# A sparse graph convolution: lists cut to groups of 32 rows, four tiles side by side, two or three tiles kept on chip

## The chip, the cores and the metric

The kernel runs on one core of a Trainium2 chip. A core has TensorE (PE in the profile, its weight loads apart as PEld), VectorE (DVE), ScalarE (ACT), GpSimd (POOL) and SyncE (SP), and 16 DMA engines that all queues share. What counts is the device time of one execution in microseconds, lower being better. Three timed runs of the kernel before gave 1521.48, 1523.54 and 1525.01; the median is 1523.54.

## The reference

One layer of a graph convolution on a dense-stored, mostly empty adjacency, with residual and layer norm; B = 8, N = 4096 nodes, F = 256 features, all fp32:

```python
HW = einsum('bnf,fo->bno', x, W)
A_norm = relu((A + A.T) * 0.5)
D = sum(A_norm, axis=1)
d = where(D > 0, D ** -0.5, 0)
L = eye(N) - d[:, None] * A_norm * d[None, :]
out = relu(einsum('nm,bmo->bno', L, HW))
return layernorm(x + out)      # mean and variance over F, eps 1e-5
```

Node n is linked to node m with a chance that falls as the root of both numbers, so the first blocks of rows are nearly dense and the last ones nearly empty; `adj` has about 70,000 entries that are not zero.

## The kernel before, in words

**Stage 1.** The adjacency is read in pairs of 512x512 blocks. PE transposes (L423), DVE adds block and transpose (L427, `sym`), ACT takes relu (L431), and DVE's reduce at L432 sums groups of 64 columns into `part`, which gives the degrees and also says which 64-row groups of the result a source row touches. The symmetric block is written to `a_dram`. Beside that, PE forms g = r (x W) for 128 rows at a time (transposes L521, products L532), ACT evicts it, and it goes to `g_dram`: one row of g holds all eight batches, 2048 numbers, 8 KB. The first 128 output rows (`lead`) are multiplied in this stage (L490).

**Lists.** The remaining 31 blocks of 128 output rows are made in 16 units of two blocks each (the last has one), in the order `SEQ` = 1 to 7, 0, 8 to 15. Unit u has the blocks 2u+1 and 2u+2. For each unit the kernel works out on the chip which source rows touch it. `patterns` (L192) gives each source row a code of four bits, one for each 64-row quarter of the unit. `KINDS` names the ten codes for which a unit has tiles of its own (one quarter alone, one block, two quarters), and kind 0 takes what is left over. `CAPS` says how many tiles of 128 source rows each kind has in each unit. `count` (L224) counts by matmuls with a triangle of ones, `place` (L234) turns the counts into positions on DVE and offers rows that do not fit their own kind to wider kinds (`OFFERS`), and `place_rest`, `spread`, `collect` and `index` make the final row numbers. `limit`, `base` and `kinds` are constants, filled by one POOL memset for each kind and unit (L163 to L166). The lists of the first units are made in stage 1, where `due` says after how many pairs of blocks each part is issued; the others are made in stage 2, some units ahead.

**Stage 2.** For each tile POOL issues two indirect DMAs: 128 pieces of adjacency rows (`ga`, L814) and 128 rows of g (L827) into the next of the 12 buffers of the ring (`RING`). One matmul step (L1032) multiplies the tile into its target rows, in four chunks of 512 columns. Tiles that touch only a 64-row half are 64 columns wide as weights, and two of them with different halves are put side by side in one step. In the units named in `HUB` the first 128 rows of g are not listed: that tile stays on chip (`g_hub`), and only its adjacency columns are loaded (L809). A block's result takes four PSUM banks, of the tag `b0` for a unit's first block and `b1` for its second[...]. `steps_of` (L750) orders the steps of a unit.

When the last step of a block is issued, `finish` (L907) issues ACT's eviction (L683); DVE's add to the residual (L693), statistics (L702) and inverse root (L715 to L721) come one half-width of matmul work later and its normalisation (L726) three. After a unit's first block is finished, `lists` (L952) takes two `b0` banks for the matmuls of later units' lists (L226, L227, L302, L303, L356), and DVE reads them (L184, L188, L189 and others). These two banks are the third and fourth chunk of the next unit's first block. `after(n, ...)` says how much matmul work must be issued before a piece is: n counts half-widths of 64 columns, and `run_later` (L843) counts them down. The order on each engine is the order of issue that this gives.

Of the kernel before, what the change touches and what calls it, by code (L numbers as in the profile page):

```python
# [15 lines left out]
U32 = mybir.dt.uint32  # L16

# [3 lines left out]
KINDS = [3, 1, 2, 4, 8, 12, 5, 10, 9, 6, 0]  # L21

ONE = slice(1, 5)

OFFERS = [
    (0, (1, 4), (3, 12)),
    (0, (2, 8), (3, 12)),
    (1, (1, 2), (5, 10)),
    (1, (4, 8), (5, 10)),
    (2, (1, 2), (9, 6)),  # L30
    (2, (4,), (6,)),
    (2, (8,), (9,)),
]
# [3 lines left out]
HUB = {0, 1, 3, 6, *range(8, 15)}  # L37

CAPS = [
    [2, 3, 3, 3, 2, 1, 2, 1, 2, 1, 6],  # L40
    [1, 3, 3, 3, 2, 1, 1, 1, 2, 1, 4],
    [1, 3, 3, 2, 2, 1, 2, 2, 1, 1, 3],
    [1, 3, 3, 3, 2, 1, 1, 1, 1, 1, 2],
    [1, 3, 3, 2, 2, 2, 1, 1, 1, 1, 2],
    [1, 3, 3, 2, 2, 1, 1, 1, 1, 1, 2],
    [1, 3, 3, 2, 2, 1, 1, 1, 1, 1, 1],
    [1, 3, 3, 2, 2, 1, 1, 1, 1, 0, 2],
    [1, 1, 2, 2, 2, 1, 1, 1, 2, 1, 1],
    [1, 2, 2, 2, 2, 1, 1, 1, 1, 1, 1],
    [1, 2, 2, 2, 2, 1, 1, 1, 1, 1, 1],  # L50
    [1, 2, 2, 2, 2, 0, 1, 1, 1, 1, 1],
    [1, 2, 2, 2, 2, 1, 1, 1, 1, 0, 1],
    [1, 2, 2, 2, 2, 1, 1, 1, 1, 0, 1],
    [1, 1, 2, 2, 2, 1, 1, 1, 1, 0, 1],
    [0, 4, 4, 0, 0, 0, 0, 0, 0, 0, 1],
# [4 lines left out]
def kernel(  # L60
# [37 lines left out]
    QU = 4  # L98
    HOLD = 10
    RING = 12  # L100
# [4 lines left out]
    mid = KINDS.index(4), KINDS.index(5)  # L105
# [9 lines left out]
    part = const.tile([P, NB, N // Q], F32, name="part")  # L115
# [39 lines left out]
    carry = const.tile([P, NK, NB], F32, name="carry")  # L155
# [3 lines left out]
    kinds = const.tile([P, NK], F32, name="kinds")  # L159
    limit = const.tile([P, NU, NK], F32, name="limit")  # L160
    base = const.tile([P, NU, NK], F32, name="base")
    for k in range(NK):
        nc.gpsimd.memset(kinds[:, k : k + 1], float(KINDS[k] or -1))  # L163
        for u in range(NU):
            nc.gpsimd.memset(limit[:, u, k : k + 1], float(CAPS[u][k] * P))
            nc.gpsimd.memset(base[:, u, k : k + 1], float(first[u][k] * P + 1))  # L166

    own = const.tile([P, QU, 2], F32, name="own")
    nc.vector.memset(own, 0.0)
    for s in range(QU):  # L170
        h = slice((s % 2) * Q, (s % 2 + 1) * Q)
        nc.vector.memset(own[h, s, s // 2 : s // 2 + 1], 1.0)
# [19 lines left out]
    def patterns(u):  # L192

        used = ipool.tile([P, QU, NB], F32, tag="used", name=f"used_{u}", bufs=1)
        nb = blocks(u)
        if nb == 1:
            nc.vector.memset(used, 0.0)
        lo = (2 * u + 1) * 2
        nc.vector.tensor_scalar(
            used[:, : 2 * nb],  # L200
            part[:, :, lo : lo + 2 * nb].rearrange("p m s -> p s m"),
            0.0,
            None,
            ALU.is_gt,
        )
        diag = used[:, :, 2 * u + 1 : 2 * u + 1 + nb]
        nc.vector.tensor_tensor(diag, diag, own[:, :, :nb], ALU.max)
        two = ipool.tile([P, 2, NB], F32, tag="two", name=f"two_{u}", bufs=1)
        uv = used.rearrange("p (b h) m -> p b h m", b=2)
        nc.vector.scalar_tensor_tensor(two, uv[:, :, 1], 2.0, uv[:, :, 0], ALU.mult, ALU.add)  # L210
        pat = ipool.tile([P, NB], F32, tag="pat", name=f"pat_{u}")
        nc.vector.scalar_tensor_tensor(pat, two[:, 1], 4.0, two[:, 0], ALU.mult, ALU.add)
        if u in HUB:
            nc.vector.memset(pat[:, :1], 0.0)
        kind = ipool.tile([P, NK, NB], BF16, tag="kind", name=f"kind_{u}")
        nc.vector.tensor_tensor(
            kind,
            pat.unsqueeze(1).to_broadcast([P, NK, NB]),
            kinds.unsqueeze(2).to_broadcast([P, NK, NB]),
            ALU.is_equal,  # L220
        )
        plan[u] = pat, kind
# [6 lines left out]
    def at_once(*kinds):  # L229

        at = [KINDS.index(k) for k in kinds]
        return slice(at[0], at[-1] + 1, at[-1] - at[0] or 1)

    def place(u, tot, low):  # L234

        pat, kind = plan[u]
        pos, incl = scan(tot, low, NK * NB, f"k{u}")  # L240
        yield
        pos = pos.rearrange("p (k m) -> p k m", k=NK)

        n = ONE.stop - ONE.start
        total = ipool.tile([P, NK], F32, tag="total", name=f"total_{u}", bufs=1)
        nc.vector.tensor_copy(total, incl.rearrange("p (k m) -> p k m", k=NK)[:, :, NB - 1])
        free = ipool.tile([P, NK], F32, tag="free", name=f"free_{u}", bufs=1)
        nc.vector.tensor_tensor(free, total, limit[:, u], ALU.min)
        nc.vector.tensor_add(free, free, base[:, u])
        nc.vector.tensor_tensor(total, total, limit[:, u], ALU.max)  # L250
        ends = ipool.tile([P, NK], F32, tag="ends", name=f"ends_{u}", bufs=1)
        nc.vector.tensor_add(ends, base[:, u], limit[:, u])
        upto = ipool.tile([P, 4, n], F32, tag="upto", name=f"upto_{u}", bufs=1)
        nc.vector.tensor_copy(upto[:, 0], limit[:, u, ONE])
# [858 lines left out]
```

## Time and profile before

| what | value |
|---|---|
| timed runs, median of 3 (lowest to highest) | 1523.54 us (1521.48 to 1525.01) |
| profiled execution: span from first to last instruction | 1527.5 us |
| stage 1 / stage 2 within it | 0 to 594.9 / 594.9 to 1514.2 us, then the last block's end |
| PE, PEld busy | 1441.2, 763.6 us |
| DVE busy | 983.6 us |
| ACT, POOL busy | 369.0, 682.0 us |
| DMA | 564.50 MB in 216714 packets, mean 370 GB/s |
| gathers and other POOL DMAs (queue q0) | 304.94 MB, 50.4% of 16 engines' span |
| matmuls of stage 2 (L1032) | 2872 records as g,ga and 176 with the kept tile |
| indirect gathers of g (L827) and of a (L814) | 268 each, 1101 and 1090 ns on POOL |

The profile is of one execution, and its span is 4 us above the median of the timed ones. Busy time of PE is not PE at its peak: matmuls are pipelined, and their ends are modelled, so neighbours overlap in the records.[...]

### The profile page before, as it was taken

To read this page: it belongs to the slowest core of one execution; us is meant where nothing else is said; L and a number is where in the kernel's file an instruction comes from. 1 tells how busy PE (TensorE), PEld (TensorE's weight loads), DVE (VectorE), ACT (ScalarE), POOL (GpSimd) and SP (SyncE) were. 2 spreads that over 40 slices of the span, in tenths; PEclk is the share of its full clock that TensorE was granted. 3 is DMA by queue.
4 is the path that set the end of the run, shared out by engine and by line. 5 is a ranking of instruction groups with operands and counts; after the bars stand their busy time and mean duration, and the time that the engine had idled before them with its cause. 6 is when DMAs were issued, how large, how long until landed. Compare 5 with 4: busy or idle time off the path is not lost.

```text
span 1527.5 us, 19332 instructions
## 1 busy us (share of the span) xinstructions
PE 1441.2 (94%) x6440; PEld 763.6 (50%) x6440; DVE 983.6 (64%) x3015; ACT 369.0 (24%) x462; POOL 682.0 (45%) x1051
## 2 busy tenths in 40 slices
PE   5999999989989989999999999999999999999995
PEld 5778777767767754433343343333433433333331
DVE  4676578888646463055568769569137688898534
ACT  3655554535434450010100100100010010001111
POOL 3002010010303316666667666666556676656653
PEclk9999999989999999999999999999999999999998
DMA  9999999999879898999999999999979999999995
GB/s 340 365 366 401 393 379 365 359 369 354 344 248 367 332 390 354 401 395 418 361 393 372 402 409 365 393 403 389 384 278 406 346 394 403 405 393 366 379 405 195
DMA packets 216714, 564.50 MB, mean 370 GB/s; under 512 B 16550, under 2 KB 104918, under 8 KB 180134
## 3 DMA queue, kind: packets, MB, share of 16 engines
q0 software_dynamic: 54224, 304.94, 50.4%
q1 hardware_dynamic: 93472, 126.89, 23.8%
q10 hardware_dynamic: 68912, 131.37, 22.7%
q8 instruction: 54, 0.88, 0.2%
q14 instruction: 52, 0.43, 0.1%
HBM read 443.61 MB, written 136.34 MB: 380 GB/s over the span
## 4 chain that ended last, share of the span: by engine, by line
PE 68%; DMA 14%; DVE 9%; issue 5%; POOL 2%; ACT 2%; ACTq 0%; DVEq 0%; POOLq 0%
PE py L1032 49%; PE pg L532 8%; DMA g<-g_dram,gi 6%; PE lead L490 5%; DMA a_dram<-sym 5%; DVE sym L427 3%; PE xtr L521 2%; PE tr L423 2%; DVE part L432 2%; DMA xin<-in_x_dram 2%; DMA ga<-a_dram,ai 1%; ACT sym L431 1%; PE lists L356 1%; ACT xt L522 1%; POOL g L827 0%
## 5 line engine op out<-in xcount | busy, mean ns | idle before, releaser
L1032 PE MATMUL py<-g,ga 128*64 128x512 f32 (+1 forms) x2872 | 813.0, 600 | 18.4 <-DMA g<-g_dram,gi 8.0
L1032 PEld LDWEIGHTS py<-g,ga 128*64 128x64 f32 (+1 forms) x2872 | 293.1, 151 | 525.1 <-issue 493.1
L827 POOL DMA_INDIRECT g<-g_dram,gi x268 | 294.9, 1101 | 219.1 <-PE py L1032 79.1
L814 POOL DMA_INDIRECT ga<-a_dram,ai x268 | 292.0, 1090 | 109.5 <-issue 76.8
L683 ACT ACTIVATE y<-py,minus_r 128x512 f32<-128x512 f32 x120 | 79.9, 687 | 812.3 <-PE py L1032 659.8
L693 DVE TENSOR_TENSOR xr<-xr,y 128x2048 f32<-128x2048 f32 x31 | 71.1, 2294 | 269.1 <-ACT y L683 267.2
L532 PE MATMUL pg<-w_sb,xt 128*128 128x256 f32 x1024 | 232.0, 385 | 5.2 <-ACT xt L522 5.2
L427 DVE TENSOR_TENSOR sym<-tr,adj 128x512 f32<-128x512 f32 x256 | 162.7, 683 | 96.9 <-PE tr L423 80.2
L532 PEld LDWEIGHTS pg<-w_sb,xt 128*128 128x128 f32 x1024 | 195.6, 194 | 33.4 <-ACT xt L522 5.6
L432 DVE TENSOR_REDUCE part<-sym 128x32 f32<-128x2048 f32 x64 | 145.5, 2279 | 62.0 <-ACT sym L431 62.0
L423 PE MATMUL tr<-ident,adj 128*128 128x128 f32 x1024 | 138.4, 285 | 30.6 <-DVE sym L427 19.2
L431 ACT ACTIVATE sym<-sym 128x2048 f32<-128x2048 f32 x64 | 122.6, 1916 | 129.9 <-DVE sym L427 117.5
L452 POOL TENSOR_TENSOR r<-e,neg_half 128x4 f32<-128x4 f32 x8 | 8.3, 1039 | 317.9 <-DVE e L451 236.5
L423 PEld LDWEIGHTS tr<-ident,adj 128*128 128x128 f32 x1024 | 118.6, 146 | 60.4 <-DVE sym L427 32.1
L521 PE MATMUL xtr<-ident,xin 128*128 128x128 f32 x512 | 72.4, 288 | 18.0 <-DVE sym L427 16.5
L702 DVE BATCH_NORM_STATS2 stats<-xr 128x6 f32<-128x256 f32 x256 | 87.0, 413 | 1.1
L726 DVE TENSOR_SCALAR xr<-xr,mv,root 128x256 f32<-128x256 f32 x248 | 83.6, 409 | 0.1
L490 PE MATMUL lead<-gt,strip 128*128 128x512 f32 x176 | 83.0, 598 | 0.0
L522 ACT COPY xt<-xtr 128x512 f32<-128x512 f32 x128 | 68.1, 591 | 46.7 <-PE xtr L521 46.0
L542 ACT ACTIVATE gt<-pg,r 128x512 f32<-128x512 f32 x88 | 60.6, 688 | 74.8 <-PE pg L532 72.3
L1032 PE MATMUL py<-g_hub,ga 128*128 128x512 f32 x176 | 77.3, 592 | 0.0
L521 PEld LDWEIGHTS xtr<-ident,xin 128*128 128x128 f32 x512 | 59.0, 146 | 34.9 <-DVE sym L427 26.4
(142 smaller groups left out, 825.8 us busy)
## 6 DMA issues: line engine op xcount, KB each, us to landing
adj<-in_adj_dram SPq DMA_DIRECT2D x64, 1024.0 KB
a_dram<-sym ACTq DMA_DIRECT2D x64, 1024.0 KB
out_dram<-xr SPq DMA_DIRECT2D x31, 1024.0 KB
xr<-in_x_dram ACTq DMA_DIRECT2D x29, 1024.0 KB
xin<-in_x_dram SPq DMA_DIRECT2D x44, 512.0 KB
g_dram<-gt ACTq DMA_DIRECT2D x22, 1024.0 KB
xin<-in_x_dram POOLq DMA_DIRECT2D x20, 512.0 KB
g_dram<-held ACTq DMA_DIRECT2D x10, 1024.0 KB
```

The source lines that it names most:

```text
L423: ins = nc.tensor.transpose(pt[:, c * P : (c + 1) * P], tji[:, c, a * P : (a + 1) * P], ident)
L427: nc.vector.tensor_add(sym[:, a, :], pt, tij[:, a, :])
L431: nc.scalar.activation(sym, sym, AF.Relu, scale=0.5)
L432: nc.vector.tensor_reduce(part[:, i * A : (i + 1) * A, j * S // Q : (j + 1) * S // Q], sym.rearrange("p a (c q) -> p a c q", q=Q), AX.X, A ...
L490: nc.tensor.matmul(lead[c], lhsT=strip, rhs=g[:, c * S : (c + 1) * S], start=not done, stop=len(done) == NB - 1, skip_group_check=True,)
L521: nc.tensor.transpose(pt[:, k, c, :], xin[b // H][:, b % H + k, c * P : (c + 1) * P], ident)
L532: ins = nc.tensor.matmul(pg[:, k * FO : (k + 1) * FO], lhsT=xt[:, b + k, c, :], rhs=w_sb[:, c, :], start=(c == 0), stop=(c == FC - 1),)
L702: nc.vector.bn_stats(stats[:, b, :], z[:, b, :])
L726: nc.vector.tensor_scalar(z[:, b, :], z[:, b, :], mv[:, b, 0:1], rstd[:, b : b + 1], ALU.subtract, ALU.mult,)
L814: nc.gpsimd.indirect_dma_start(out=at if both else at[:, :P], out_offset=None, in_=a_pairs if both else a_rows, in_offset=bass.IndirectOff ...
L827: nc.gpsimd.indirect_dma_start(out=gt, out_offset=None, in_=g_dram, in_offset=bass.IndirectOffsetOnAxis(ap=gi[:, t : t + 1], axis=0), boun ...
L1032: nc.tensor.matmul(py[2 * u + 1 + b][c][rows, :], lhsT=at[:, off + rows.start : off + rows.stop], rhs=gt[:, c * S : (c + 1) * S], start=ne ...
```

## The change

A unit's lists now go down to groups of 32 rows. There are eight groups in a unit, a source row's code has eight bits, and there are 15 kinds: one group alone (eight of them, 1 to 128), a block (15, 240), two 64-row halves (51, 204, 60, 195) and 0 for the rest. A tile of a single group has 32 columns as weights, and four of them, one for each group of a block, make one step. `CAPS` is new for every unit. `HUBS` says for each unit how many of the first tiles of g (128 rows each) stay on chip: three, two, or none in the last unit. The ring has 11 buffers instead of 12, the pool of adjacency rows 14 as before (`RING` + 3), and kept tiles take no buffer of the ring: `gather_ahead` issues gathers until the ring is full. In stage 1 `keep` sums groups of 32 columns (`sums`), marks which are not zero (`uses`, one byte each) and sums again to `part`, one number for each row and 512 columns. `patterns` works out the code of eight bits, the code of four halves and the code of two blocks. `place` offers rows in two rounds of operations on all eight single kinds. `steps_of` begins a unit with four-wide steps and tiles of its first block, then mixes kept tiles, half pairs and the rest, and ends with the second block's own. `run_later` counts widths down in 64ths as before, a 32-column matmul as half.

```diff
-KINDS = [3, 1, 2, 4, 8, 12, 5, 10, 9, 6, 0]
...
-OFFERS = [
-    (0, (1, 4), (3, 12)),
-    (0, (2, 8), (3, 12)),
-    (1, (1, 2), (5, 10)),
-    (1, (4, 8), (5, 10)),
-    (2, (1, 2), (9, 6)),
-    (2, (4,), (6,)),
-    (2, (8,), (9,)),
-]
+KINDS = [15, 1, 4, 2, 8, 16, 64, 32, 128, 240, 51, 204, 60, 195, 0]
...
-HUB = {0, 1, 3, 6, *range(8, 15)}
+HUBS = [3] * 4 + [2] * 11 + [0]
...
 CAPS = [
-    [2, 3, 3, 3, 2, 1, 2, 1, 2, 1, 6],
...
+    [2, 2, 1, 2, 1, 1, 1, 1, 1, 2, 1, 1, 1, 2, 5],
+    [2, 2, 2, 1, 1, 1, 1, 2, 2, 1, 1, 1, 1, 1, 3],
+    [1, 1, 2, 2, 1, 2, 1, 1, 2, 1, 1, 1, 1, 1, 2],
+    [1, 1, 1, 1, 1, 1, 1, 1, 1, 1, 1, 1, 1, 1, 2],
+    [1, 1, 1, 2, 2, 2, 2, 1, 1, 1, 1, 1, 1, 1, 1],
+    [1, 1, 1, 2, 2, 1, 1, 1, 1, 1, 1, 1, 1, 1, 1],
+    [1, 1, 1, 1, 1, 1, 1, 1, 1, 1, 1, 1, 1, 1, 1],
+    [1, 1, 1, 2, 2, 2, 1, 1, 1, 1, 1, 1, 0, 1, 1],
+    [0, 1, 1, 1, 1, 1, 1, 1, 1, 1, 1, 1, 1, 0, 2],
+    [1, 1, 1, 1, 1, 1, 1, 1, 1, 1, 1, 1, 1, 0, 1],
+    [1, 1, 1, 1, 1, 1, 1, 1, 1, 1, 1, 1, 1, 0, 1],
+    [1, 1, 1, 1, 1, 1, 1, 1, 1, 1, 0, 0, 1, 0, 2],
+    [0, 1, 1, 1, 1, 1, 1, 1, 1, 1, 1, 1, 1, 0, 1],
+    [1, 1, 1, 1, 1, 1, 1, 1, 1, 1, 1, 1, 0, 0, 1],
+    [1, 1, 1, 1, 1, 1, 1, 1, 1, 1, 0, 0, 0, 0, 2],
+    [1, 2, 2, 2, 2, 0, 0, 0, 0, 0, 0, 0, 0, 0, 0],
...
     Q = 64
-    QU = 4
+    E = 32
+    QU = P // E
+    NE = 2 * QU
     HOLD = 10
-    RING = 12
+    RING = 11
     EPS = 1e-5
     NK = len(KINDS)
     tiles = [sum(caps) for caps in CAPS]
     first = [[sum(caps[:k]) for k in range(NK)] for caps in CAPS]
-    mid = KINDS.index(4), KINDS.index(5)
+    mid = KINDS.index(16), KINDS.index(51)
+    NL = NK - 1
     tmax = max(tiles)
 
...
-    part = const.tile([P, NB, N // Q], F32, name="part")
+    uses = const.tile([P, NB, N // E], U8, name="uses")
+    part = const.tile([P, NB, NS], F32, name="part")
...
-    kinds = const.tile([P, NK], F32, name="kinds")
-    limit = const.tile([P, NU, NK], F32, name="limit")
-    base = const.tile([P, NU, NK], F32, name="base")
-    for k in range(NK):
-        nc.gpsimd.memset(kinds[:, k : k + 1], float(KINDS[k] or -1))
+    kinds = const.tile([P, NL], F32, name="kinds")
+    limit = const.tile([P, NU, NL], F32, name="limit")
+    base = const.tile([P, NU, NL], F32, name="base")
+    singles, pairs, whole = slice(1, 1 + NE), slice(10, 14), slice(0, 10, 9)
+    codes = [1, *KINDS[singles], 2, 17, 68, 20, 65]
+    for k in range(NL):
+        nc.gpsimd.memset(kinds[:, k : k + 1], float(codes[k]))
         for u in range(NU):
             nc.gpsimd.memset(limit[:, u, k : k + 1], float(CAPS[u][k] * P))
             nc.gpsimd.memset(base[:, u, k : k + 1], float(first[u][k] * P + 1))
...
     def patterns(u):
 
-        used = ipool.tile([P, QU, NB], F32, tag="used", name=f"used_{u}", bufs=1)
+        def t(shape, name, dtype=F32, **kw):
+            return ipool.tile(shape, dtype, tag=name, name=f"{name}_{u}", **kw)
+
+        def weave(out, pairs_of, by):
+            nc.vector.scalar_tensor_tensor(out, pairs_of[:, :, 1], by, pairs_of[:, :, 0], ALU.mult, ALU.add)
+
+        used = t([P, NE, NB], "used", bufs=1)
         nb = blocks(u)
         if nb == 1:
             nc.vector.memset(used, 0.0)
-        lo = (2 * u + 1) * 2
-        nc.vector.tensor_scalar(
-            used[:, : 2 * nb],
-            part[:, :, lo : lo + 2 * nb].rearrange("p m s -> p s m"),
-            0.0,
-            None,
-            ALU.is_gt,
+        lo = (2 * u + 1) * QU
+        nc.vector.tensor_copy(
+            used[:, : QU * nb], uses[:, :, lo : lo + QU * nb].rearrange("p m s -> p s m")
         )
         diag = used[:, :, 2 * u + 1 : 2 * u + 1 + nb]
         nc.vector.tensor_tensor(diag, diag, own[:, :, :nb], ALU.max)
-        two = ipool.tile([P, 2, NB], F32, tag="two", name=f"two_{u}", bufs=1)
-        uv = used.rearrange("p (b h) m -> p b h m", b=2)
-        nc.vector.scalar_tensor_tensor(two, uv[:, :, 1], 2.0, uv[:, :, 0], ALU.mult, ALU.add)
-        pat = ipool.tile([P, NB], F32, tag="pat", name=f"pat_{u}")
-        nc.vector.scalar_tensor_tensor(pat, two[:, 1], 4.0, two[:, 0], ALU.mult, ALU.add)
-        if u in HUB:
-            nc.vector.memset(pat[:, :1], 0.0)
-        kind = ipool.tile([P, NK, NB], BF16, tag="kind", name=f"kind_{u}")
-        nc.vector.tensor_tensor(
-            kind,
-            pat.unsqueeze(1).to_broadcast([P, NK, NB]),
-            kinds.unsqueeze(2).to_broadcast([P, NK, NB]),
-            ALU.is_equal,
-        )
+        if HUBS[u]:
+            nc.vector.memset(used[:, :, : HUBS[u]], 0.0)
+        several = t([P, NB], "several", bufs=1)
+        nc.vector.tensor_reduce(several, used.rearrange("p s m -> p m s"), AX.X, ALU.add)
+        two = t([P, QU, NB], "two", bufs=1)
+        weave(two, used.rearrange("p (b h) m -> p b h m", h=2), 2.0)
+        four = t([P, 2, NB], "four", bufs=1)
+        weave(four, two.rearrange("p (b h) m -> p b h m", h=2), 4.0)
+        pat = t([P, NB], "pat")
+        nc.vector.scalar_tensor_tensor(pat, four[:, 1], 16.0, four[:, 0], ALU.mult, ALU.add)
+        nc.vector.tensor_scalar(two, two, 1.0, None, ALU.min)
+        ones_q = t([P, 2, NB], "ones_q", bufs=1)
+        weave(ones_q, two.rearrange("p (b h) m -> p b h m", h=2), 4.0)
+        quarter = t([P, NB], "quarter", bufs=1)
+        nc.vector.scalar_tensor_tensor(quarter, ones_q[:, 1], 16.0, ones_q[:, 0], ALU.mult, ALU.add)
+        nc.vector.tensor_scalar(four, four, 1.0, None, ALU.min)
+        block = t([P, NB], "block", bufs=1)
+        nc.vector.scalar_tensor_tensor(block, four[:, 1], 2.0, four[:, 0], ALU.mult, ALU.add)
+        nc.vector.scalar_tensor_tensor(block, several, 1.0, block, ALU.is_gt, ALU.mult)
+        kind = t([P, NL, NB], "kind", BF16)
+        for ks, code in ((singles, pat), (pairs, quarter), (whole, block)):
+            n = kinds[:, ks].shape[1]
+            nc.vector.tensor_tensor(
+                kind[:, ks],
+                code.unsqueeze(1).to_broadcast([P, n, NB]),
+                kinds[:, ks].unsqueeze(2).to_broadcast([P, n, NB]),
+                ALU.is_equal,
+            )
         plan[u] = pat, kind
...
+        upto = ipool.tile([P, 3, NE], F32, tag="upto", name=f"upto_{u}", bufs=1)
+        nc.vector.tensor_copy(upto[:, 0], limit[:, u, singles])
+        off = ipool.tile([P, 3, NE], F32, tag="off", name=f"off_{u}", bufs=1)
+        nc.vector.tensor_copy(off[:, 0], base[:, u, singles])
+
+        def by_place(a):
+            return a.rearrange("p (b r i) -> p r i b", b=2, r=2)
+
+        def offer(s, at, to):
+            has, shift = by_place(upto[:, s]), by_place(off[:, s + 1])
+            then = by_place(upto[:, s + 1])
+            left, end, wants = free[:, to], ends[:, to], by_place(total[:, singles])
+            has, shift, then, wants = (a[at] for a in (has, shift, then, wants))
+            if len(at) == 2:
+                left, end = (a.rearrange("p (b i) -> p i b", b=2) for a in (left, end))
+            nc.vector.tensor_sub(shift, left, has)
+            nc.vector.tensor_sub(then, end, shift)
+            nc.vector.tensor_tensor(then, then, wants, ALU.min)
+            nc.vector.tensor_add(left, then, shift)
+
+        every = slice(None)
+        for h in range(2):
+            offer(0, (every, h), pairs)
+        for h in range(2):
+            for i in range(2):
+                offer(1, (every, h, i), whole)
...
         def keep(i, j, sym, diag):
             nc.scalar.activation(sym, sym, AF.Relu, scale=0.5)
-            nc.vector.tensor_reduce(
-                part[:, i * A : (i + 1) * A, j * S // Q : (j + 1) * S // Q],
-                sym.rearrange("p a (c q) -> p a c q", q=Q),
-                AX.X,
-                ALU.add,
+            rows = slice(i * A, (i + 1) * A)
+            sums = stat1.tile([P, A, S // E], F32, tag="sums", name=f"sums_{i}_{j}")
+            nc.vector.tensor_reduce(sums, sym.rearrange("p a (c q) -> p a c q", q=E), AX.X, ALU.add)
+            nc.vector.tensor_scalar(
+                uses[:, rows, j * S // E : (j + 1) * S // E], sums, 0.0, None, ALU.is_gt
             )
+            nc.vector.tensor_reduce(part[:, rows, j], sums, AX.X, ALU.add)
...
+        def side_by_side(*kinds):
+            n = max(len(of[k]) for k in kinds)
+            return [[(k, of[k][c]) for k in kinds if c < len(of[k])] for c in range(n)]
+
+        pairs = side_by_side(51, 204) + side_by_side(60) + side_by_side(195)
+        rows = side_by_side(0)
+        held = [[(0, -1 - h)] for h in range(HUBS[u])]
+        n = max(len(held), len(pairs), len(rows))
+        mixed = [s for c in range(n) for s in held[c : c + 1] + pairs[c : c + 1] + rows[c : c + 1]]
+        return (
+            side_by_side(1, 2, 4, 8)
+            + side_by_side(15)
+            + mixed
+            + side_by_side(240)
+            + side_by_side(16, 32, 64, 128)
+        )
 
...
-        tc.tile_pool(name="rows", bufs=RING + 2) as apool,
+        tc.tile_pool(name="rows", bufs=RING + 3) as apool,
...
-        for n in range(RING):
-            gather(n)
-        n = RING
+        asked = eaten = done_tiles = 0
+
+        def gather_ahead():
+            nonlocal asked
+            while asked < len(order):
+                fetched = len(ring_tiles)
+                if asked - done_tiles >= RING + 2 or (order[asked][2] >= 0 and fetched - eaten >= RING):
+                    break
+                gather(asked)
+                asked += 1
+
+        gather_ahead()
...
-            for k, t in step:
-                gather(n)
-                n += 1
-            run_later(sum(1 + (rows == slice(0, P)) for _, rows, _, _ in work))
+            done_tiles += len(step)
+            eaten += sum(t >= 0 for _, t in step)
+            gather_ahead()
+            run_later(sum((rows.stop - rows.start) / Q for _, rows, _, _ in work))
```

## The prediction, made before the changed kernel was run

> **What bounds the kernel now.** I read the page's busy shares first, then its costliest groups, then the span cut into stages, then the instructions at single unit changes. From the page (engine rows: busy tenths in 40 slices; groups: busy us, mean ns, idle before and what ended it):
>
> ```profile
> span 1527.5 us, 19332 instructions
> ...
> PE   5999999989989989999999999999999999999995
> DVE  4676578888646463055568769569137688898534
> DMA  9999999999879898999999999999979999999995
> ...
> L1032 PE MATMUL py<-g,ga 128*64 128x512 f32 (+1 forms) x2872 | 813.0, 600 | 18.4 <-DMA g<-g_dram,gi 8.0
> ...
> L432 DVE TENSOR_REDUCE part<-sym 128x32 f32<-128x2048 f32 x64 | 145.5, 2279 | 62.0 <-ACT sym L431 62.0
> ```
>
> TensorE and the DMA engines are both near full. Stage 2 by groups of units (window, its length, busy and count of PE, PEld, DVE, ACT, POOL, then clock, DMA share, GB/s):
>
> ```profile
> 594.90:1040.70 445.80, 435.86 (x1733) 166.14 (x1734) 283.41 (x1074) 36.38 (x56) 299.61 (x277) 0.99 1.01 392
> 1040.70:1145.50 104.80, 104.80 (x360) 40.98 (x358) 44.57 (x173) 5.04 (x8) 61.90 (x60) 1.00 0.92 344
> 1145.50:1345.30 199.80, 199.28 (x851) 76.09 (x850) 163.12 (x634) 21.56 (x33) 134.64 (x119) 1.00 1.00 389
> 1395.60:1514.20 118.60, 112.86 (x418) 41.38 (x414) 62.15 (x217) 13.69 (x21) 61.33 (x58) 0.99 0.94 359
> ```
>
> PE is busy 98% there and the DMA share is 1.0 outside unit 0 (the second line). The first matmul starts of a step are 429 ns apart though each is recorded as 592 ns, so a slot (one tile, or one set of tiles side by side, four chunks of 512 columns in two passes) costs 8 x 0.429 = 3.43 us. Counted from the caps in the code: 250 slots x 3.435 = 859 us; list matmuls 16 x 1.24 = 20; the rest of the 919.3 us of stage 2, about 40, is waiting: some 7 for DVE to read the lists' banks, 33 for tiles.
>
> How a unit change looks when only one step stands between the lists and the next unit, units 11 to 12, on PE and on DVE (start, length, what):
>
> ```profile
> 1340.93 0.95 PE L356 MATMUL lists<-val,hot 128*128 128x28 bf16 x32
> 1341.81 5.37 PE L1032 MATMUL py<-g,ga 128*64 128x512 f32 x24
> 1349.35 1.59 PE L1032 MATMUL py<-g,ga 128*64 128x512 f32 x4 [2.17 <-DVE pos_k L188]
> ```
>
> ```profile
> 1337.96 2.29 DVE L693 TENSOR_TENSOR xr<-xr,y 128x2048 f32<-128x2048 f32 x1 [4.46 <-ACT y L683]
> ...
> 1348.78 0.52 DVE L188 TENSOR_TENSOR pos_k<-incl_k,lists 128x352 f32<-128x352 f32 x1
> 1349.33 0.52 DVE L189 TENSOR_TENSOR pos_k<-pos_k,lists 128x352 f32<-128x352 f32 x1
> ```
>
> The first block's last matmul is at 1336.6; add, statistics, root and list reading end on DVE at 1349.85, 13.2 us later. The two banks of the lists are chunks 2 and 3 of the next unit's first block, so its first step took 6.7 us instead of 3.43: 3.2 lost.
>
> In stage 1 DVE is full in the middle:
>
> ```profile
> 215.00:365.00 150.00, 135.94 (x735) 105.61 (x734) 132.55 (x390) 69.55 (x80) 9.41 (x20) 0.95 0.99 360
> 240.00:280.00 40.00, 38.70 (x207) 28.96 (x206) 39.09 (x134) 18.44 (x23) 0.00 (x0) 1.00 1.00 364
> ```
>
> At the start DVE stands behind POOL's memsets of constants, from the list of waits (total, times, longest):
>
> ```profile
> DVE ends L252 <- POOL base L166: 12.2, 1, 12.2
> ```
>
> **What the Trainium skill says.** "TensorE: Matmul & The Clock Gate", Measured speedup vs the span model: tiles placed side by side start about 4 ns apart and three 32-column tiles gave 2.38 times. The trace of before has pairs only: their matmuls start 7 ns apart and a pair takes one tile's time; four are not shown. "VectorE: DVE Perf Modes", The TRN2 errata: an fp32 tensor_tensor takes (N+151)/0.96 ns; the trace agrees (512 columns: 691 against 0.684 us; 352: 524 against 0.52). "DMA: Bandwidth & Descriptors", Issuing engines are not separate DMA queues: the trace agrees in so far as POOL's gathers and the other queues together fill the same 16 engines to 1.0.
>
> **The change part by part.** *Stage 1, constants.* 14 listed kinds instead of 11, each 1 + 2x16 memsets: 462 instead of 363. They run one every 34 ns, and the `ends` of the first unit waits for number 433 instead of 334: +3.4 us ahead of the first `sym`. DMA drops to 220 GB/s at 15-20 us since no buffer comes free, so I count all 3.4.
> *Stage 1, DVE.* `keep` gains a tensor_scalar and a small reduce (rows of like size 0.17-0.26 with overlap: about 0.4 together) x64 = 26 us, of which 18 lie in 215-365: 7. `patterns` there, four times, is about 16 operations for 7: +1.8 each = 7; `place` has 24 small operations for 28 but 448-wide rows for 352 (+0.1 each) and 256-wide for 128 (+0.13): +0.65 x4 = 2.6. Together 17 into a stretch with 17.5 us idle on DVE, but less than 1 us idle of each 40 in the two full parts, which make up over half of it. I charge 10.5 of 17; ends: 4 and 17. Before 215 DMA and after 365 PE hide the rest; without that cover the other 46 x 0.4 = 18 us would show.
> *Stage 2, slots.* By the new caps: 252 gathered tiles for 268, 34 uses of kept tiles for 11, 241 slots for 250: -9 x 3.43 = -31 us, if four tiles cost what one does.
> *Stage 2, DMA.* Rows gathered plus kept tiles loaded: 29,634+384 for 32,174+128 rows of 8 KB: -18.7 MB, adjacency tiles +0.8 MB: at 387 GB/s -46 us of transfer. It shows only as shorter waits for tiles, since PE is the fuller engine: PE's work is then 828+20, transfers about 862. I take 33 to 25 us, -8. Against it stand a ring of 11 and steps that need four tiles at once: the first step starts two gathers (2.6 us each on POOL) later.
> *Stage 2, list reading.* The lists go out when two half-widths have run after the first block's end. Before, three steps mostly follow that end (one of kind 12, two pairs), so two stand between lists and next unit: the 13.2 us chain is just covered by 3x3.43+1.24+1.7 (two chunks) = 13.3. After, at the ends of units 3, 5, 6 and 8 to 12, kind 240 and one four-wide step follow: one stands between, and the cover is 9.8. The chain grows by 0.4 (448 columns in three operations). Stall 3.2 to 3.8 at each of eight changes, less the one existing: 8x3.5-3.2 = +25. Reads queue behind L693 and root, and the out-normalise behind them; nothing on PE waits for that. Ends: 0 if DVE gets there sooner, 30.
> *Stage 2, DVE.* Busy about 42 of the 46-53 us of a late unit; +2.5 to 4 (patterns, reading) brings it to the 46 of a 13-slot unit: +4, ends 0 and 20.
> Sum: 3.4+10.5-31-8+25+4 = +4 on the profiled 1527.5, 1531. That execution's span is 4 us over the median of the timed runs, 1523.5; so 1528 for the median.
>
> **The rivals.** (a) *Faster: the stalls replace waits for tiles.* Gathers go on while PE stands at a list reading, so 28 us of standing and 46 us less transfer can leave almost no wait for tiles: 33 to 5, -28 instead of -8; with stage 1's operations falling into gaps (4 instead of 10.5) the sum is 3.4+4-31-28+25+4 = -23: 1500. Its place is the ring between POOL's gathers and PE; it decides once waits for tiles fall under 18 us, where the sum reaches -3. For it: transfers of 862 us against 828+20+28 of PE. Against: the ring holds 11 tiles, under three four-wide steps, and DMA was already at a share of 1.0 beside a full PE. (b) *DVE becomes the bound* of stage 1's middle (all 17) and of units 8 to 14 (20): +27, 1549. For: 39.1 of 40 busy. Against: DVE idles in earlier units. (c) *Slower by tiles: four tiles do not run as one.* About 37 steps are four wide; at two at a time they add 37 x 3.43 = 127, part of it in place of tile and list waits: +60 to +100, 1590-1625. It decides from 0.1 of a slot (13 us) on. The skill's 2.38 of 3 would make it 0.26 x 37 x 3.43 = 33, 1560. (d) *Nothing moves*: savings and stalls cancel to within 0.2%, about 3 us, which is what a measurement here can tell.
>
> **Numbers.** My forecast (1515-1541) 0.44, (a) 0.28, (b) 0.18, (c) 0.10. Within 0.2% come 0.13 from the lower part of the forecast's own range and from (d), which lies in it; faster 0.26 of (a) and 0.06 of the forecast = 0.32; slower the rest, 0.55. Range 1500 to 1556: it takes in (a)'s centre and (b).
>
> **What would show it.** Matmul starts of a four-wide step some 7 ns apart in fours, 429 ns to the next four, or else (c). Idle PE before chunks 2 and 3 of units 4, 6, 7 and 9 to 13, ended by `pos_k`; if it is there and gather waits are under 18 us, (a). The first `sym` at 18 instead of 14.6 us; stage 1 ending near 609 instead of 595; stage 2 near 909 us. Waits for tiles above 33 us in stage 2, or DVE at 100% in units 8 to 14, would make the forecast too low.

## The result, and the profile after

The changed kernel takes 1547.37 us (median of four runs, 1545.46 to 1549.99) where before takes 1523.27 (1521.48 to 1525.01): a ratio of 1.0162, 95% interval 1.0141 to 1.0183. It is 24 us slower. The forecast was 1528 in a range of 1500 to 1556; the sign was right, the size (24 us for 4) was not.

The page of the changed kernel, its rows and groups as before:

```profile
span 1543.8 us, 19779 instructions
...
PE   5999998989897989899999999999999999999994
...
DMA  8999999999988899978998999999968999999995
...
L1067 PE MATMUL py<-g,ga 128*32 128x512 f32 (+2 forms) x2600 | 638.5, 613 | 32.2 <-DMA g<-g_dram,gi 19.0
...
L1067 PE MATMUL py<-g_hub,ga 128*128 128x512 f32 x544 | 239.2, 593 | 0.0
```

More of the matmuls use kept tiles (544 records for 176). Idle time ahead of the step's matmuls is longer, 32.2 us for 18.4, and most of it ends with a gather of g. Gathered and kept bytes fell from 304.94 to 287.61 MB on the gathers' queue, and the mean rate from 370 to 354 GB/s with them: fewer bytes, in more time.

Stage 2 by groups of units, columns as in the prediction:

```profile
613.50:1070.10 456.60, 441.56 (x1838) 168.82 (x1838) 302.52 (x1109) 39.17 (x57) 309.63 (x278) 0.99 0.95 360
1070.10:1172.70 102.60, 101.58 (x360) 42.81 (x364) 43.06 (x164) 4.76 (x7) 54.21 (x54) 0.98 0.84 315
1172.70:1373.50 200.80, 194.49 (x846) 75.95 (x841) 175.74 (x656) 21.97 (x33) 131.24 (x118) 0.98 1.00 385
...
1418.50:1530.40 111.90, 103.78 (x412) 39.45 (x404) 65.50 (x236) 13.71 (x21) 62.40 (x57) 0.94 0.96 372
```

Stage 1 ends at 613.5 instead of 594.9: +18.6. Stage 2 takes 916.9 instead of 919.3: -2.4. What lies behind it is 13.4 in both. The nine saved slots (31 us) are gone inside stage 2. Counted from the caps, none of them is in units 1 to 7 (121 slots for 120): unit 0 has two fewer, units 8 to 15 eight. In units 1 to 7 and in unit 0 the DMA share has dropped (0.95 and 0.84; it was 1.01 and 0.92): here bytes were saved while PE was the fuller engine. In units 8 to 11, on the third line, it is 1.00.

The waits that carry this, from the lists of waits of the changed kernel (total, times, longest), and from its timeline the start of stage 2 on PE:

```profile
PE py L1067 <- DMA g<-g_dram,gi: 19.0, 12, 2.6
...
PEld py L1067 <- DVE pos_k L183: 16.4, 7, 3.5
DVE ends L253 <- POOL base L161: 16.0, 1, 16.0
```

```profile
617.26 3.59 PE L1067 MATMUL py<-g,ga 128*32 128x512 f32 x26 [1.68 <-DMA g<-g_dram,gi]
622.93 1.02 PE L1067 MATMUL py<-g,ga 128*32 128x512 f32 x2 [2.07 <-DMA g<-g_dram,gi]
626.39 8.14 PE L1067 MATMUL py<-g,ga 128*32 128x512 f32 x19 [2.45 <-issue]
```

The first two steps of unit 1 take 11.6 us over their two slots; in before they started without a wait.

The two profiled executions are 16.3 us apart, the medians 24. A run of the changed kernel with a span of 1543.8 is listed at 1545.46 us, so the profiled execution of before (span 1527.5) stands for about 1529, 6 above its median, and that of the changed kernel 2 below its own. Three kernels below that have the stage 2 of before, untouched, spent 909.0, 911.2 and 912.7 us in it where the profiled execution of before spent 919.3: units 2, 3 and 7 were longer in it (7 in two of the three comparisons), so its waits for tiles there were probably unlucky ones.

### The profile page after: what moved, and what is told of

The parts are those of the page before. It is cut to its first block, busy times and chain, and to the rows that moved or that the text cites. A ratio compares the mean times of both kernels' runs of the same rounds, so it can differ in the third digit from the quotient of the medians.

```text
span 1543.8 us, 19779 instructions
## 1 busy us (share of the span) xinstructions
PE 1428.1 (93%) x6536; PEld 764.4 (50%) x6536; DVE 1038.3 (67%) x3199; ACT 370.9 (24%) x462; POOL 686.6 (44%) x1143
## 3 DMA queue, kind: packets, MB, share of 16 engines
q0 software_dynamic: 52512, 287.61, 47.7%
## 4 chain that ended last, share of the span: by engine, by line
PE 47%; DMA 24%; issue 14%; DVE 8%; POOL 5%; ACT 2%; ACTq 0%; POOLq 0%; DVEq 0%
PE py L1067 31%; DMA g<-g_dram,gi 14%; PE pg L549 7%; DMA ga<-a_dram,ai 4%; DMA a_dram<-sym 3%; PE tr L439 3%; DVE sym L443 2%; PE lead L507 2%; PE xtr L538 2%; POOL ga L840 2%; POOL g L853 2%; DVE sums L450 2%; ACT sym L447 1%; DMA xin<-in_x_dram 1%; DMA g_dram<-held 1%
## 5 line engine op out<-in xcount | busy, mean ns | idle before, releaser
L1067 PE MATMUL py<-g,ga 128*32 128x512 f32 (+2 forms) x2600 | 638.5, 613 | 32.2 <-DMA g<-g_dram,gi 19.0
L1067 PEld LDWEIGHTS py<-g,ga 128*32 128x32 f32 (+2 forms) x2600 | 224.2, 140 | 432.3 <-issue 386.8
L853 POOL DMA_INDIRECT g<-g_dram,gi x252 | 289.3, 1148 | 204.2 <-PE py L1067 99.8
L840 POOL DMA_INDIRECT ga<-a_dram,ai x252 | 284.9, 1130 | 117.0 <-issue 73.0
L1067 PE MATMUL py<-g_hub,ga 128*128 128x512 f32 x544 | 239.2, 593 | 0.0
L450 DVE TENSOR_REDUCE sums<-sym 128x64 f32<-128x2048 f32 x64 | 145.3, 2277 | 58.8 <-ACT sym L447 58.8
L1067 PEld LDWEIGHTS py<-g_hub,ga 128*128 128x128 f32 x544 | 103.2, 190 | 130.8 <-issue 127.2
L497 POOL DMA_DIRECT2D xin<-in_x_dram x20 | 15.2, 762 | 155.8 <-PE xtr L538 139.7
## 6 DMA issues: line engine op xcount, KB each, us to landing
xin<-in_x_dram SPq DMA_DIRECT2D x44, 512.0 KB, 10.4
g_dram<-held ACTq DMA_DIRECT2D x10, 1024.0 KB, 11.6
```

Of the source, the lines that this page charges most:

```text
L450: nc.vector.tensor_reduce(sums, sym.rearrange("p a (c q) -> p a c q", q=E), AX.X, ALU.add)
L840: nc.gpsimd.indirect_dma_start(out=at if both else at[:, :P], out_offset=None, in_=a_pairs if both else a_rows, in_offset=bass.IndirectOff ...
L853: nc.gpsimd.indirect_dma_start(out=gt, out_offset=None, in_=g_dram, in_offset=bass.IndirectOffsetOnAxis(ap=gi[:, t : t + 1], axis=0), boun ...
L1067: nc.tensor.matmul(py[2 * u + 1 + b][c][rows, :], lhsT=at[:, off + rows.start : off + rows.stop], rhs=gt[:, c * S : (c + 1) * S], start=ne ...
```

## The experiments

Experiments 1, 5, 6 and 8 ran on a chip on which before took 1531.0 us, experiments 2, 3 and 7 beside a before of 1524.4 and the others beside one of 1523.4; so ratios to before are compared, not times. The edits are shown shortened.

**1. The memsets in unit order.**

```diff
-    for k in range(NL):
-        nc.gpsimd.memset(kinds[:, k : k + 1], float(codes[k]))
-        for u in range(NU):
+    for u in SEQ:
+        for k in range(NL):
+            if u == SEQ[0]:
+                nc.gpsimd.memset(kinds[:, k : k + 1], float(codes[k]))
```

> The changed kernel with the same 462 memsets in another order: all constants of the first unit first, then unit by unit. Theory: DVE's first sym waits for the memset of the first unit's last constant, so it starts soon after the first transposes (7.8 us) instead of at 18.8, the gap of the DMA engines at 17 to 22 us closes, and about 9 us are saved: 1538. Rival: the start is bound by DMA or the loss is made up later; then only 0 to 4 us are saved, 1543 to 1547.

Measured: 1548.17 us, ratio 1.0109 (1.0092 to 1.0126), against 1.0162 of the changed kernel: 0.53% of 1531 or 8 us, with intervals that leave some 4 us either way. From the timeline of DVE in this run:

```profile
3.42 0.17 DVE L254 TENSOR_TENSOR ends<-base,limit 128x14 f32<-128x14 f32 x1 [0.89 <-POOL base L162]
...
8.88 0.69 DVE L444 TENSOR_TENSOR sym<-tr,adj 128x512 f32<-128x512 f32 x1 [0.96 <-PE tr L440]
```

The gate is gone: the first `sym` waits for PE at 8.88 us instead of for a memset until 18.8. But the trace keeps less of it than the ratio: against before, the 41st `sym` is 0.7 us late instead of 5.2, the 249th 15.2 instead of 17.6, and stage 2 starts at 610.8 instead of 613.5. The gate is shown; its worth is some 3 us by the trace and 8 by the times, which differ by no more than the intervals allow.

**2. The same edit in before.**

> The kernel before with its 363 memsets in unit order, first unit first. Theory: before has the same gate, at 14.6 us instead of 18.8; its first sym comes at about 8.6 and 5 us are saved. Rival: e1 gained by something else than the gate; then nothing here.

Measured: 1520.36 us, ratio 0.998 (0.9967 to 0.9992), 3 us. The first `sym` comes at 8.7 us, 5.9 earlier; at 17 us the lead is 2.6, from 80 us on 0.8 to 1.9. So of a gate of 6 us a third or less lasts. This is the fastest version seen: its interval ends just below the time of before.

**3. `keep` alone, in before.**

```diff
-            nc.vector.tensor_reduce(part[...], sym by 64, AX.X, ALU.add)
+            nc.vector.tensor_reduce(sums, sym by 32, AX.X, ALU.add)
+            nc.vector.tensor_scalar(uses, sums, 0.0, None, ALU.is_gt)
+            nc.vector.tensor_reduce(part[...], sums by 2, AX.X, ALU.add)
```

> The kernel before with keep's new operations alone: sums of 32 columns, a comparison whose result nothing reads, and the sums of 64 from them; lists and stage 2 as before. Theory: of the +10 us between 220 and 350 us about half is keep's two extra operations, so 4 to 7 us slower than before. Rival: the list operations are all of it and keep's fall into gaps: within 2 us of before.

Measured: 1531.44 us, ratio 1.0048 (1.0032 to 1.0063), 7 us. In its trace `sym` falls back by 1.2 to 1.8 us up to 222 us, by 4.8 at 357, and stage 2 starts at 600.4 instead of 594.9. The rival (within 2 us) is out: two small operations on each of 64 blocks cost some 5 us by the trace and 5 to 10 by the interval of the times. One difference to the changed kernel remains: here the sums are kept in buffers that `patterns` and the list making use too (`used`, `way`), so part of it could be waiting for them; that was not tried apart.

**4. The list operations alone, in before.** `patterns` of the first four units gets ten more operations that work on `used` and whose results nothing reads.

```diff
+            for out in (x[:, 64:320], x[:, 64:320]):
+                nc.vector.scalar_tensor_tensor(out, wide, 2.0, wide, ALU.mult, ALU.add)
+            nc.vector.tensor_reduce(x[:, :32], x[:, 64:320] by 8, AX.X, ALU.add)
+            for n in (128, 64, 32, 32, 32):
+                nc.vector.scalar_tensor_tensor(x[:, :n], row[:, :n], 2.0, row[:, :n], ALU.mult, ALU.add)
+            for n in (128, 64):
+                nc.vector.tensor_scalar(x[:, :n], row[:, :n], 1.0, None, ALU.min)
```

> The kernel before with ten idle DVE operations in patterns of the first four units, 2.8 us a unit, like those that the change adds; their results are not used. Theory: DVE's list operations stand on the path in stage 1, so all of the 11 us show: stage 2 starts 8 to 11 us later and before becomes 8 to 11 us slower. Rival: a gap takes them, under 4 us; then the rest of the 19 us of stage 1 has another cause.

Measured: 1525.6 us, ratio 1.0008 (0.9991 to 1.0025); the trace shows stage 1 3.8 us longer. The theory that list operations show in full fell; the rival, under 4 us, held. What differs in the changed kernel is seen at 230 us of its own PE timeline:

```profile
237.84 3.71 PE L439 MATMUL tr<-ident,adj 128*128 128x128 f32 x16 [6.14 <-DVE sym L443]
```

Here DVE runs some twenty operations, most of them of `patterns` and one a reduce of 2.28 us, between two `sym`; PE waits 6.14 us for the next one. The longest such gap at that place in before is 2.37 us:

```profile
229.90 0.85 PE L423 MATMUL tr<-ident,adj 128*128 128x128 f32 x4 [2.37 <-DVE sym L427]
```

In this experiment the idle operations hang on nothing and the order put many of them singly between `sym` operations. That the position makes the difference is the reading of these two orders; it was not tried apart.

**5. List making of the first units later.**

```diff
-            if i == 1:
+            if i == 2:
                 for n, u in enumerate(SEQ[:2]):
...
-            elif i == 2:
+            elif i == 3:
                 for n, u in enumerate(SEQ[2:4]):
...
-            elif i < 5 and i > 2:
+            elif i < 6 and i > 3:
```

> The changed kernel with patterns and list making of the first four units in stage 1 issued one row of blocks later each (work moved from about 220-370 us to about 290-460 us, none removed). Theory: it is DVE's extra work in the stretch where DVE is full that costs the +10 us between 220 and 350 us; where PE and DMA bind, it is hidden, so some 6 to 10 us are saved: 1539. Rival: keep's two extra operations on each block cost it, or DVE is as full later; then under 3 us are saved.

Measured: 1554.96 us, ratio 1.0161 (1.0144 to 1.0178): nothing. Windows of this kernel (first fence) and of the changed kernel as it ran beside experiment 7 (second):

```profile
220.00:300.00 80.00, 76.36 (x432) 60.65 (x431) 58.75 (x114) 41.22 (x47) 4.23 (x9) 1.00 1.04 391
...
360.00:420.00 60.00, 49.70 (x246) 38.21 (x247) 43.42 (x150) 23.86 (x29) 10.45 (x18) 0.86 0.82 292
```

```profile
220.00:300.00 80.00, 69.39 (x367) 53.30 (x367) 72.30 (x214) 35.10 (x41) 4.33 (x9) 0.94 0.92 332
...
360.00:420.00 60.00, 54.28 (x291) 43.06 (x290) 45.67 (x103) 29.93 (x37) 11.62 (x19) 0.94 0.98 367
```

Without list making the stretch from 220 to 300 us runs faster: the 145th `sym` is 1.9 us ahead of before instead of 11.7 behind. With it the stretch from 360 to 420 runs slower, and all is lost again by 410 us, although DVE is busy only 43.4 of 60 us there. So list making costs where it stands, and not only where DVE is full. Its last pieces now stand in the last row of blocks, where the last `sym` comes 9.5 us later than in the changed kernel; stage 1 ends at 621.7 us instead of 613.5. The move thus added a cost of its own at the end, and the equal times are no clean measure of what was won before.

**6. Lists' banks read before the statistics.**

```diff
             def rest():
                 z = xr.pop(i)
                 with queue("dve"):
-                    mv, var = moments(i, y, z, stat)
+                    nc.vector.tensor_add(z, z, y)
+                if i % 2 == 1:
+                    after(3.5, middle, z)
+                else:
+                    middle(z)
+
+            def middle(z):
+                with queue("dve"):
+                    mv, var = statistics(i, z, stat)
```

> The changed kernel with the statistics and the inverse root of a unit's first block issued after the reading of the lists' banks on DVE (the add stays where it was). Theory: the 28 us in which PE waits for pos_k at unit changes fall to under 6 and the time falls by about 20: 1527. Rival: the waits for tiles grow by as much, since the gathers lose the time in which they ran ahead; then under 8 us are saved, 1540 or more.

Measured: 1555.91 us, ratio 1.0154 (1.0128 to 1.0179): no gain. `pos_k` stalls fell to 5.9 us on the weight loads, but there is a wait that the changed kernel hasn't, from the list of waits:

```profile
DVE xr L953 <- DMA xr<-in_x_dram: 42.0, 6, 11.3
```

The late normalisation holds the residual's buffers, so its next rows are loaded late, and 23 us lie between the last matmul step and the end instead of 13. The two effects can't be told apart here; hence the next experiment.

**7. The same, mended.**

```diff
-                if i % 2 == 1:
-                    after(3.5, middle, z)
+                if i % 2 == 1 and i < NB - 8:
+                    after(2.5, middle, z)
...
-                after(3, end)
+                after(1 if i % 2 == 1 and i < NB - 8 else 3, end)
```

> As e2_read_first, but the statistics wait half a width more only (2.5 instead of 3.5), the normalisation follows them at once, and the last units are left as they were: e2 had DVE's adds wait 42 us for late loads of the residual rows, whose buffers its late normalisation held. Theory: with these loads back in time, the shorter stalls at unit changes show, 8 to 15 us under the changed kernel on this chip. Rival: the waits for tiles take all of it, under 4 us.

> The changed kernel itself, as the yardstick for the runs beside it on this chip. Expected 1.016 times before. In its trace stage 2 should again be as long as that of before within 5 us, and stage 1 about 18 us longer.

Measured: 1546.26 us, ratio 1.015 (1.0116 to 1.0183); the changed kernel beside it 1546.86, 1.0148 (1.0111 to 1.0185). The changed kernel's stage 1 is 20 us longer than before's (614.5), its stage 2 919.1, as expected. Units 11 and 13 in this experiment (first) and in the changed kernel of the result (second):

```profile
1317.70:1364.30 46.60, 46.60 (x203) 19.29 (x198) 44.33 (x167) 5.56 (x9) 32.65 (x29) 1.00 1.02 390
...
1408.10:1455.20 47.10, 44.60 (x198) 17.38 (x194) 29.25 (x105) 5.19 (x9) 29.62 (x29) 1.00 1.03 400
```

```profile
1322.90:1373.50 50.60, 48.39 (x202) 19.38 (x197) 45.29 (x170) 5.49 (x9) 29.93 (x28) 0.97 0.97 370
...
1418.50:1461.60 43.10, 42.86 (x199) 17.03 (x194) 29.75 (x107) 5.48 (x9) 27.85 (x27) 1.00 1.02 399
```

No wait for `pos_k` is left. Unit 11 now takes 46.6 us, its 13 slots and the lists' matmuls, instead of 50.6, and PE is busy in all of it. But unit 13 takes 47.1 instead of 43.1 at a DMA share of 1.03: what the first steps of units 4, 6, 7 and 9 to 12 won (16 us), the waits for gathers in those of units 13 and 14 took back by half (8 us). The mend is not complete: DVE still waits 22 us for residual rows in units 13 and 14. Stage 2 is 9.4 us shorter than in the changed kernel beside it (909.7 against 919.1), stage 1 of that execution 4.4 us longer for no reason that the edit gives, and the timed runs are 0.6 us apart, less than they scatter. So the rival, under 4 us, held in time. The stall was real and its removal shortens stage 2 of this trace, but no gain in time was shown.

**8. The first unit's steps in another order.**

```diff
-            side_by_side(1, 2, 4, 8)
-            + side_by_side(15)
-            + mixed
+            side_by_side(15) + mixed + side_by_side(1, 2, 4, 8)     # for SEQ[0] alone
```

> The changed kernel with the steps of the first unit alone in another order: block tiles and mixed steps first, the four-wide steps of the first block after them. Theory: the 12 us that the first unit takes longer than before are PE starving for four tiles at once at the start of stage 2; a step of one tile and two slots needs a quarter of the tiles for the same PE time, so 9 us are saved: 1538. Rival: the tiles come late in any order, the waiting is put off to the later steps of the unit; under 3 us saved.

Measured: 1558.85 us, ratio 1.0178 (1.0155 to 1.02): the rival. Unit 1 takes 88.5 us instead of 92.3, unit 2 78.2 instead of 71.7. The tiles come late in any order. What limits them there isn't settled: the DMA share of unit 1 is 0.85 and POOL is busy 59 of 92.5 us.

**9. Four-wide steps as two two-wide steps.**

```diff
-            side_by_side(1, 2, 4, 8)
+            side_by_side(1, 2)
+            + side_by_side(4, 8)
...
-            + side_by_side(16, 32, 64, 128)
+            + side_by_side(16, 32)
+            + side_by_side(64, 128)
```

> The changed kernel with every four-wide step as two steps of two (1 with 2, 4 with 8, 16 with 32, 64 with 128): the same tiles and bytes, 40 slots more, one step more between the lists and the next unit. Theory: four tiles run as one, so 40 x 3.43 = 137 us of PE come in, less the stalls at unit changes (20 us) and most of the waits for tiles (some 35 us): about 80 us slower than the changed kernel, near 1627. Rival: the four share something and gain little over pairs; then within 30 us of the changed kernel.

Measured: 1585.63 us, ratio 1.0402 (1.0363 to 1.0441), 39 us over the changed kernel: the direction of the theory at half its size, and over the rival's 30. The theory had the stalls for list reading vanish, but PE waits 14.2 us for `pos_k` where the changed kernel waits 10.4; the waits for gathers did fall, from 19.0 us to 3.3. The last section says where the other half is.

**10 and 11. Fewer kept tiles, early and late.**

```diff
-HUBS = [3] * 4 + [2] * 11 + [0]
+HUBS = [3] + [1] * 3 + [2] * 11 + [0]      # early; kind 0 gets two tiles more in units 1 to 3
+HUBS = [3] * 4 + [1] * 11 + [0]            # late; kind 0 gets one tile more in units 4 to 14
```

> The changed kernel with one kept tile of g instead of three in units 1 to 3, and two more tiles of kind 0 in each: six gathers of 1 MB more, the same slots. Theory: in these units PE is the bound and the DMA share only 0.86 to 0.95, so bytes saved there buy nothing: within 4 us of the changed kernel. Rival: every MB counts, 6 x 1.1 MB at 387 GB/s, less the kept tile that is then loaded later: 15 us slower.

> The changed kernel with one kept tile instead of two in units 4 to 14, and one tile of kind 0 more in each: eleven gathers of 1 MB more, the same slots. Theory: units 4 to 14 are full on DMA (share 1.0 at 390 GB/s), so the bytes count there: 11 x 1.1 MB at 387 GB/s = 31 us less what the stalls at unit changes hide, 15 to 30 us slower than the changed kernel. Rival: PE and the unit changes bind there too; under 5 us.

Measured: early 1547.75 us, ratio 1.0153 (1.0135 to 1.0171), the same as the changed kernel; late 1567.65, ratio 1.0279 (1.0261 to 1.0297), 20 us over it. Unit 3 of the early run and of the changed kernel, then unit 13 of the late run:

```profile
778.00:842.80 64.80, 64.80 (x264) 25.56 (x260) 41.90 (x156) 5.86 (x9) 42.70 (x39) 1.00 0.97 378
```

```profile
777.50:842.40 64.90, 64.90 (x267) 25.61 (x262) 42.22 (x155) 5.96 (x9) 41.14 (x37) 1.00 0.91 353
```

```profile
1426.70:1479.40 52.70, 47.32 (x196) 18.01 (x193) 29.33 (x105) 5.52 (x9) 32.70 (x31) 0.94 1.01 385
```

In unit 3 two gathers more are moved in the same 64.9 us, at 378 instead of 353 GB/s: PE is the bound. In unit 13 one gather more and the late tiles of the units ahead cost 9.6 us (the granted clock, 0.94, is in that figure too). Both theories held.

## Why the prediction was right or wrong

Against the profiled execution of before, by the prediction's own terms:

| term | predicted | measured |
|---|---|---|
| constants | +3.4 | +4.2 at the first `sym` |
| DVE in stage 1 | +10.5 | the rest of +18.6, 14 |
| slots | -31 | -31 (nine by count, 3.43 us each) |
| list reading | +25 | +15.5 |
| waits for tiles | -8 | +13 |
| DVE in stage 2 | +4 | none seen |
| sum | +4 | +16 |

The measured terms for list reading and for tiles come from the start of each step: what steps took over their slots of 3.43 us sums to 61 us before and 89.5 after, about 20 of each for the lists' matmuls; of the other 28.4 more, 15.5 lie in first steps that wait for list reading, 13 in the rest.

That the change came out slower is in part luck. With list reading at its measured 15.5 and all else as predicted the sum would have been -6, faster than before; a miss of 9.5 one way was covered by one of 21 the other way.

**Slots: right.** In a four-wide step of the changed kernel (the run beside experiment 7) the four matmuls start at 1173.239, .245, .252 and .259 us and the next four at 1173.668: 7 ns apart, and 429 ns to the next. Rival (c), that four tiles do not run as one, is out. Its 37 steps are 32 of four tiles, and 8 more that experiment 9 also splits in two; what those 40 are worth, experiment 9 gives: 39 us, and not 40 slots of 3.43. The 2.38 of three that the Trainium skill gives for 32-column tiles ("TensorE: Matmul & The Clock Gate", Measured speedup vs the span model), from which 1560 was worked out, is not what a steady stream of fp32 matmuls does here: four take the time of one.

**Constants: right** in place and size; experiments 1 and 2 show the gate, and their traces that a good part of such a delay is made up later.

**DVE in stage 1: right in place, too small.** 14 instead of 10.5, near the upper end of 17 that was kept for it. To charge only what falls into the stretch from 215 to 365 us was wrong: experiment 5 moved list making to where DVE is busy 43 of 60 us, and what had been won was lost there. `keep` has some 5 of it by the trace (experiment 3), idle list operations of equal length 1 to 4 (experiment 4). The other 5 to 8 us stay open: they may hang on where the operations of `patterns` stand among the `sym`, which no run tried by itself.

**List reading: the mechanism right, the size not.** The first steps of units 4, 6, 7 and 9 to 12 take 2.4, 2.7, 2.4, 1.7, 4.0, 3.6 and 1.9 us over a slot: 18.8, less the 3.3 of unit 12 before. Six changes of eight cost less than the 3.5 that one example gave. The first step of unit 10, one of the two that cost more, has its wait here, on PE:

```profile
1276.08 7.17 PE L1067 MATMUL py<-g,ga 128*32 128x512 f32 x24 [2.58 <-DVE pos_k L183]
```

The two, and the example itself (unit 12 of before), have something in common that no term names: right after the wait the granted clock is one half for 3.41 us. Windows of unit 10 in the changed kernel, then of unit 12 in before:

```profile
1275.97:1279.38 3.41, 3.30 (x16) 0.59 (x16) 3.38 (x11) 0.00 (x0) 2.50 (x4) 0.50 1.04 381
```

```profile
1349.79:1353.20 3.41, 3.41 (x10) 0.95 (x8) 3.41 (x10) 0.00 (x0) 2.23 (x3) 0.50 1.06 407
```

Matmul starts are about 854 ns apart in both instead of 429. Counted from the starts, that makes 1.3 of the 4.0, 1.1 of the 3.6 and 0.8 of the 3.3; the rest of the slow stretch falls into the next step. Experiments 2, 3 and 4 have the stage 2 of before and the same wait at unit 12, of 2.1 to 2.3 us. Where the slow stretch follows it (before and experiment 4) the unit takes 50.3 and 50.2 us, where none follows (2 and 3) 48.6: 1.7 less, which is half of 3.41. So the example was dear in part by chance, and eight times its price was too much. In experiment 7 the seven first steps are 2.9 us over their slots in all.

**Waits for tiles: the step that failed.** "PE's work is then 828+20, transfers about 862. I take 33 to 25 us" set the saved bytes against stage 2 as a whole, and took 8 us off waits that instead grew by 13; by the account above they are about 51 us (38 before), where the prediction had named 33 as the mark above which its forecast would be too low. Bytes were saved where PE is the bound: the DMA share is 0.84 to 0.94 in units 1 to 3 and 0, and 0.97 to 1.04 in units 4 to 14. Six gathers more in units 1 to 3 cost nothing, eleven more in units 4 to 14 cost 20 us (experiments 10 and 11). Unit 1 starves 11.6 us at its start (a lead of two gathers, about 5 us, had been reckoned for that), unit 15, whose two four-wide steps want eight tiles within two slots, 16.3 instead of 9.9. Why the tiles come late in unit 1 stays open (experiment 8). And the waits of before were probably an unlucky draw by about 8 us, to judge by the three other kernels with its stage 2; that is also the difference between 16 and the 24 of the medians.

Part of this is again the clock. In stage 2 of the changed kernel the granted clock was 0.50 for 30.7 us, in six stretches, each of which follows a wait of PE of 2.0 to 2.6 us; in before it was so for 13.7 us. PE was busy in 24.9 and 13.0 of them, so some 12 and 6 us went to slow matmuls (an estimate, half of the busy time). Of the 28 us more over the slots about 6 are then slow work after waits and not the waits themselves, some 2 of them with list reading and 4 with waits for tiles.

**The rivals.** (a) wanted the stalls to stand in for waits for tiles; both were there at once, 18.8 beside more waits than before. (b) names about the time that came, but not its way: DVE is not the bound of units 8 to 14, for in experiment 7 units 9 to 12 run at their slots with DVE as busy as ever (44.6 of 46.9 us). Its half in stage 1, 17 us, is near what happened, 14.

## What to carry to other kernels

Set saved bytes and saved matmuls against each other stretch by stretch: here six gathers more cost nothing where the matmuls are the bound, and eleven more cost 20 us where the DMA engines are full. Where two engines are nearly full, don't book the whole of a stall as gain: here half of what was removed on PE came back as waits for gathers. Small operations can cost time even in a stretch where their engine has idle time. Before one stall is taken as the price of eight, look at the granted clock beside it; and waits read from one profiled execution can be off by several us, so look at a second one where one is to be had.

## What was not expected of the hardware

Narrow steps that follow each other on other columns overlap. In experiment 9 a step of one 32-column tile starts matmuls at 705.784, 706.213, 706.642 and 707.071 us; from its fifth on, at 707.500, two of the next step start beside each of its own (707.506 and .513, then 707.930, .960 and .966, and so on every 429 ns). So the next step begins after four starts, 1.72 us, where a full slot has eight; which start belongs to which step is read from this pattern. With 281 slots of 3.43 us stage 2 would have lasted 964 us without any wait or list; it lasted 951.4. Taken in order of their starts, the steps of experiment 9 that are shorter than their slots save 61 us in all. That, less what stalls remained against the theory, is why pairs cost 39 us and not 80. A forecast in whole slots overstates what four-wide steps are worth over such pairs; the pairs of before fill all 128 columns, so the nine slots saved against it are not touched by this.
